# Attention with a gated layer: layernorm statistics gathered at a slot's start, one sum formed last, the output weights' sums moved to VectorE, half of the sigmoids formed later

## The chip, the cores and the metric

The kernel runs on one core of a Trainium2 chip. The metric is the device time of one execution in microseconds (us); lower is better. The kernel before was timed three times: 1114.41, 1114.5 and 1115.24 us, so the median is 1114.5 us.

## The reference

All in float32, for 4 rows of 512 tokens with 1024 features:

```python
xn = layernorm(x)                                   # no weight, no bias
q, k, v = xn @ Wq, xn @ Wk, xn @ Wv                 # 16 heads of 64; rotary on q and k
a = softmax(causal(q @ k.T) / 8) @ v
s = a @ Wo
routing = softmax(xn @ gate_w.T)                    # 8 experts
f = ((xn * (routing @ in_scale)) @ sign(weight).T) * (routing @ out_scale) + bias
out = x + s * silu(f)
```

## The kernel before, in words

**Strassen products.** Every large product is split into 2x2 blocks and done with seven block products instead of eight. For that the kernel forms sums of blocks: `form_w` (S1 to S4, of weights) and `form_x` (T1 to T4, of a row's normalized input X) for the projections, `form_a` (S1 to S4 of attention's output) and `sum_wo` (t1 to t4 of the output weights `wo`) for the output projection, `sign_sum` (T1 to T4 of the sign weights) for the gated layer. They are done on VectorE (DVE), except t3, which GpSimd (POOL) forms: `engine = nc.gpsimd if n == 3 else nc.vector` (L995). T1 of the last row is written in place over the block b12 of X, since no other place is left; the rows before have a place of their own.

**Two halves.** The first half of the program does the projections and the attention of 16 groups (4 rows b times 4 groups g), in 16 *slots*. Slot k projects group k in 84 steps (a step is one `nc.tensor.matmul`, which is two MATMUL rows in the trace), and into these steps the attention of group k-1 is woven, as a list of 16 *pieces* (`attention_pieces`, `interleave`): one piece each 5.25 steps. A group has two units, u0 and u1. The plan of pieces: 4: values of an older unit, scores of u0 and softmax of its tiles 1 and 3; 6: softmax of u0's tiles 2 and 0; 10: `transpose_blocks(u0)`; 12: values, then scores and first softmax of u1; 14: the rest of u1's softmax; 2 of the next slot: `transpose_blocks(u1)`. In the slots of g = 2 and g = 3 the next row's layernorm is woven in too: tile t0's whole layernorm at the slot's first piece, tile t0+1's at piece 7, TensorE transposes of t0 at pieces 8 and 9, of t0+1 at 13 and 14. The x tiles have two buffers; the fourth tile of a row is loaded at piece 15 of the slot of g = 2, once the buffer of tile t0+1 has been transposed.

A layernorm is two `bn_stats` (L171), `bn_aggr` (L177), a square root on ScalarE (ACT, L179), a reciprocal and the normalization on DVE (L186, L187). ACT holds one set of function tables at a time: a square root after an exponential has an ACT_TABLE_LOAD before it, and so has the next exponential.

`softmax` adds the mask (L542) and takes the maximum (L545) on DVE, exponentiates on ACT (L548), and scales on POOL (L558). `transpose_blocks` is ten transposes on DVE from p to y (L576, "the burst"), pinned in a row, and 16 DMAs from y back to p (L586), all on SyncE's (SP) queue for most units. `values` multiplies by v (L601), copies the result on ACT (L610) and stores it to at_d. `rotary` is four ACT copies (L316, L317), one DVE operation (L318) and two POOL operations (L319, L320), after the last add of a projection (`c`, L349).

**The second half** starts at L961. With the last two units still in work, the gated layer of the token pairs q = 0 and 1 (`gated`, `ffn`) is computed in pieces by `dense`, which also issues `sum_wo`; `gate` (L1021, L1022) multiplies and adds the bias, and `silu` (L1029, L1030) is a sigmoid on ACT and a product on POOL. All eight `silu` of q = 0 and 1 stand ahead of the loop over pairs. The loop does for each q: `form_a` (for q < 2), then `project_out(q)`, whose products come in the order 1 (a11 by b11), 6 (S2 by t2), 2, 7 (S3 by t3), 5 (S1 by t1), 4 (by t4), 3. It stops at four `yield`s: ahead of product 1, after product 6, after product 7, after product 5; at each, one entry of the list `ahead` is issued. For q = 0 these are the sign sums 1, 2, 3.

**What sets the order.** The order on TensorE (PE) is the program's. On the other engines a planner orders the instructions of each engine by its own estimate of when they are ready, with program order as the priority; `keep_in_program_order` pins an instruction behind the one that was issued before it on its engine. Each engine runs its list strictly in order, so a waiting instruction holds all behind it. TensorE's results lie in a ring of four PSUM banks (`bank`), shared by projections, transposed x, tile 1's scores and values; a bank is free when its readers on DVE or ACT are done.

Of the kernel before, what the change touches and what calls it, by code (L numbers as in the profile page):

```python
# [9 lines left out]
F32 = mybir.dt.float32  # L10
F32R = mybir.dt.float32r
AF = mybir.ActivationFunctionType
ALU = mybir.AluOpType
# [7 lines left out]
B, S, E = 4, 512, 1024  # L21
# [21 lines left out]
def attn_gated_ffn_kernel(  # L43
# [138 lines left out]
    def normalize(b, t):  # L182
        xt = xin[b, t]
        mv, std = MV[b, t]
        rstd = st.tile([P, 1], F32, tag="rstd", name=f"rstd_{b}_{t}")
        nc.vector.reciprocal(rstd, std)  # L186
        nc.vector.tensor_scalar(xt, xt, mv[:, 0:1], rstd, op0=ALU.subtract, op1=ALU.mult)  # L187

    def layernorm(b, t):
        half_statistics(b, t, 0)  # L190
        half_statistics(b, t, 1)
        deviation(b, t)
        normalize(b, t)

    def transpose_x(b, t, g):
        if b not in X:
# [94 lines left out]
    def form_x(b, n):  # L291
        b11, b12, b21, b22 = quarters_x(b)
        if n > 1:
            f = fp.tile([P, 4, TH], F32, tag=f"T{n}", name=f"T{n}_{b}")
        elif b < B - 1:

            f = sgp.tile([P, 4, TH], F32, tag="last", name=f"T1_{b}")
        else:

            f = b12  # L300
        TF[b, n] = f
        x0, x1 = {
            1: lambda: (b12, b11),
            2: lambda: (b22, TF[b, 1]),
            3: lambda: (b22, b12),
            4: lambda: (b21, TF[b, 2]),
        }[n]()
        nc.vector.tensor_tensor(f, x0, x1, op=ALU.subtract)
# [534 lines left out]
    def attention_pieces(k, late):  # L843

        units = [(*groups[k], i) for i in range(2)]
        w, v = late
        u0, u1 = units

        def values_and_scores(before, u):
            def both():  # L850
                if before:
                    values(before)
                scores(u)
                softmax(u, 1, 3)

            return both

        pieces = [[] for _ in range(16)]  # L860

        last = k == len(groups) - 2
        plan = {
            2: lambda: v and transpose_blocks(v),
            3 if last else 4: values_and_scores(w, u0),
            4 if last else 6: lambda: softmax(u0, 2, 0),
            8 if last else 10: lambda: transpose_blocks(u0),
            9 if last else 12: values_and_scores(v, u1),
            10 if last else 14: lambda: softmax(u1, 2, 0),
        }  # L870
        if last:
            plan[14] = lambda: transpose_blocks(u1, ordered=True)
        for n, piece in plan.items():
            pieces[n].append(piece)
        return pieces, units
# [11 lines left out]
    for k, (b, g) in enumerate(groups):  # L887
        pieces = [[] for _ in range(9)]
        if k > 0:
            pieces, late = attention_pieces(k - 1, late)  # L890

        def at(n, piece):
            pieces[n].append(piece)


        if g == 0:
            routing = [lambda n=n: router(b, n) for n in range(3)]
            if k == 0:
                at(0, routing[0])
                at(1, lambda: (load_scales(in_scale), load_scales(out_scale)))  # L900
                at(2, routing[1])
                at(4, routing[2])
                at(5, lambda: split_scales(isc))
            else:
                if b < B - 1:
                    at(5, routing[0])
                at(8, routing[1])
                at(15, routing[2])
        elif g == 1 and b + 1 < B:

            at(11, lambda: [load_x(b + 1, t) for t in range(2)])
            if b == 0:
                at(1, lambda: split_scales(osc))
        elif g > 1 and b + 1 < B:
            t0 = 2 * (g - 2)
            layernorm(b + 1, t0)
            at(7, lambda: layernorm(b + 1, t0 + 1))
            for n, t, h in ((8, t0, 0), (9, t0, 1), (13, t0 + 1, 0), (14, t0 + 1, 1)):
                at(n, lambda t=t, h=h: transpose_x(b + 1, t, h))
            if g == 2:  # L920
                at(11, lambda: load_x(b + 1, 2))
                at(15, lambda: load_x(b + 1, 3))
        if k in (5, 9, 12, 14):
            n = {5: 0, 9: 2, 12: 4, 14: 6}[k]
            at(0, lambda: (load_sign(n), load_sign(n + 1)))
            at(8, lambda: make_sign(n))
            at(15, lambda: make_sign(n + 1))
        if b == B - 1:

            if g < 2:  # L930
                load_xn(g)
            if g in (1, 2):
                at(1, lambda: in_scales(g - 1, score_banks))
            if g == 3:
                z_place[0] = [xip.tile([P, E], F32, tag="x", name=f"z0_{i}") for i in range(2)]
                at(1, lambda: out_scales(0, score_banks))
        if k == 11:

            at(15, lambda: router(b + 1, 0))
        interleave(pieces, fill, 3 * 7 * 4 if k else 3 * 7 * 4 - 8)  # L940
        if g == NGRP - 1:
            for _ in fill:
                pass
            if b + 1 < B:
                for n in (3, 1, 2, 4):
                    form_x(b + 1, n)
                fill = projections(b + 1)
    pctx.close()
# [39 lines left out]
    def sum_wo(n, c):  # L988
        out_, x0, x1 = {
            1: (t1, b12, b11),  # L990
            2: (t2, b22, t1),
            3: (t3, b22, b12),
            4: (t4, b21, t2),
        }[n]
        engine = nc.gpsimd if n == 3 else nc.vector  # L995
        difference = engine.tensor_tensor(out_[:, c, :], x0[:, c, :], x1[:, c, :], op=ALU.subtract)  # L996
        if n != 3:
            tc.keep_in_program_order(difference)

    def ffn(q, i, k):  # L1000

# [24 lines left out]
    def silu(q, i, k):  # L1026
        z = Z[q, i][:, k * HALF : (k + 1) * HALF]
        g = work.tile([P, HALF], F32, tag="g", name=f"g_{q}_{i}_{k}")
        nc.scalar.activation(g, z, AF.Sigmoid)  # L1029
        nc.gpsimd.tensor_tensor(z, z, g, op=ALU.mult)  # L1030
# [16 lines left out]

    u0, u1 = units = [(*groups[-1], i) for i in range(2)]
    w, v = late
    sums = iter([(n, c) for n in (1, 3, 2, 4) for c in range(4)])  # L1050

    def dense(gates, n, n_sums=0):
        for i in range(n):
            next(gates)
            if i < n_sums:
                sum_wo(*next(sums))
# [7 lines left out]
    dense(gates, 8)  # L1064

    split(1, 0)
    transpose_blocks(u0, ordered=True)
    load_wo(1)
    values(v)
    scores(u1)  # L1070
# [7 lines left out]
    out_scales(1, score_banks)  # L1078
    dense(gates, 2)
    transpose_blocks(u1, (nc.sync, nc.scalar), ordered=True)  # L1080
    dense(gates, 10, 10)
    values(u0)
    dense(gates, 2, 2)
    values(u1)
    for _ in gates:
        pass
# [28 lines left out]
    def sign_sum(n):  # L1115

        if n == 3:
            TS[n] = [sg[4], sg[5]]
        else:
            t = (app if n == 4 else tsp).tile(  # L1120
                [P, 2, E], F32R, tag="ap" if n == 4 else f"T{n}", name=f"Tsg{n}"
            )
            TS[n] = [t[:, r, :] for r in range(2)]
        for r in range(2):
            x0, x1 = {
                1: lambda: (sg[4 + r], sg[r]),
                2: lambda: (sg[6 + r], TS[1][r]),
                3: lambda: (sg[6 + r], sg[4 + r]),
                4: lambda: (sg[2 + r], TS[2][r]),
            }[n]()  # L1130
            nc.vector.tensor_tensor(
                TS[n][r], x0.bitcast(F32), x1.bitcast(F32), op=ALU.subtract
            )

    PARTS = {}
# [185 lines left out]
            )  # L1321

    load_xn(2)

    for q in range(2):
        for i in range(2):
            for k in range(2):
                silu(q, i, k)
    for q in range(len(pairs)):
        if q < 2:  # L1330
            for n in range(1, 5):
                form_a(q, n)
        if q == 0:
            load_at(1)
        ahead, later = [], []
        if q == 0:
            ahead = [lambda n=n: sign_sum(n) for n in (1, 2, 3)]
        elif q < len(pairs) - 1:
            ahead = [
                lambda: None,  # L1340
                lambda: (in_scales(q + 1), later.append(first_parts(q + 1))),
                lambda: out_scales(q + 1),
                lambda: later.pop()(),
            ]
        for _ in project_out(q):
            if ahead:
                ahead.pop(0)()
        if q != 1 and q + 1 < len(pairs):
            load_at(max(q + 1, 2))
        if q == 1:  # L1350
            sign_sum(4)
        if 1 <= q < len(pairs) - 1:
            gated_by_strassen(q + 1)
            if q + 2 < len(pairs):
                load_xn(q + 2)
# [58 lines left out]
```

## Time and profile before

| | |
|---|---|
| timed runs | 1114.41, 1114.5, 1115.24 us |
| profiled execution | 1114.49 us, of which its span is 1112.6 us |
| mean granted TensorE clock | 0.998 |
| busy: PE, DVE, POOL, ACT | 98%, 81%, 52%, 42% of the span |
| ACT_TABLE_LOAD for a square root (L179) | 12, of 1283 ns each |

The profile is of one execution. In the timeline view a row is a run of like instructions of one engine: start, length, engine, line, operation, output<-inputs, shapes, count, and in brackets the idle time before it with the instruction that ended it. A wait on several semaphores is put down to the one that came last, so the name in the brackets can be wrong where that one had long been done. Ends of matmuls are modelled; the distance from start to start is the safer figure.

### The profile page before, as it was taken

To read this page: it belongs to the slowest core of one execution; us is meant where nothing else is said; L and a number is where in the kernel's file an instruction comes from. 1 tells how busy PE (TensorE), PEld (TensorE's weight loads), DVE (VectorE), ACT (ScalarE), POOL (GpSimd) and SP (SyncE) were. 2 spreads that over 40 slices of the span, in tenths; PEclk is the share of its full clock that TensorE was granted. 3 is DMA by queue.
4 is the path that set the end of the run, shared out by engine and by line. 5 is a ranking of instruction groups with operands and counts; after the bars stand their busy time and mean duration, and the time that the engine had idled before them with its cause. 6 is when DMAs were issued, how large, how long until landed. Compare 5 with 4: busy or idle time off the path is not lost.

```text
span 1112.6 us, 15955 instructions
## 1 busy us (share of the span) xinstructions
PE 1086.9 (98%) x5176; PEld 788.0 (71%) x5176; DVE 896.9 (81%) x1736; ACT 469.9 (42%) x1080; POOL 575.5 (52%) x594
## 2 busy tenths in 40 slices
PE   9999999999989999998999999999979999999998
PEld 8887677787768778776877787777744545655664
DVE  7887989788897978889787987887797777667764
ACT  2553665454366545436653452664520222122220
POOL 0672555555255555525552662674585455444535
PEclk9999999999999999999999999999999999999999
DMA  9415556644655664465566544554683222431431
GB/s 322 144 60 149 174 148 159 194 136 120 178 168 155 169 177 135 120 180 168 159 169 195 171 149 141 151 131 127 165 252 114 81 91 103 156 118 47 142 114 57
DMA packets 86898, 163.88 MB, mean 147 GB/s; under 512 B 13472, under 2 KB 49056, under 8 KB 80800
## 3 DMA queue, kind: packets, MB, share of 16 engines
q1 hardware_dynamic: 80528, 152.91, 46.2%
q0 software_dynamic: 4576, 8.39, 2.2%
q10 hardware_dynamic: 1712, 1.57, 0.5%
q8 instruction: 41, 0.67, 0.3%
q14 instruction: 41, 0.34, 0.1%
HBM read 95.45 MB, written 25.43 MB: 109 GB/s over the span
## 4 chain that ended last, share of the span: by engine, by line
PE 74%; DVE 11%; POOL 4%; issue 3%; ACT 3%; DMA 2%; SPq 1%; POOLq 0%; DVEq 0%; ACTq 0%
PE pj L335 25%; PE wo L1235 16%; PE pj L422 13%; PE ff L1175 7%; PE sc L522 5%; PE pv L601 5%; POOL p L558 2%; DVE y L576 2%; DVE S L289 2%; DVE nmx L545 1%; SPq L586 1%; PE xtp L201 1%; DVE w L289 1%; DMA xn_d<-X 1%; ACT sw L317 1%
## 5 line engine op out<-in xcount | busy, mean ns | idle before, releaser
L558 POOL TENSOR_SCALAR p<-p,rs 128x256 f32<-128x256 f32 (+3 forms) x256 | 181.8, 726 | 189.0 <-DVE rs L556 144.3
L548 ACT ACTIVATE p<-sc,nmx 128x256 f32<-128x256 f32 (+3 forms) x256 | 132.8, 529 | 92.9 <-DVE nmx L545 72.6
L319 POOL TENSOR_TENSOR sw<-sw,sin_sb 128x512 f32<-128x512 f32 x64 | 89.6, 1400 | 94.4 <-ACT sw L317 93.0
L335 PE MATMUL pj<-X,w 128*128 128x256 f32 x576 | 134.4, 382 | 0.2 <-ACT X L207 0.2
L335 PE MATMUL pj<-T,S 128*128 128x256 f32 x512 | 118.2, 381 | 8.5 <-ACT v L610 7.2
L335 PEld LDWEIGHTS pj<-X,w 128*128 128x128 f32 x576 | 108.1, 190 | 18.6 <-issue 2.9
L576 DVE STREAM_TRANSPOSE y<-p 128x256 f32<-128x256 f32 x320 | 110.2, 408 | 12.7 <-POOL p L558 12.7
L316 ACT ACTIVATE sw<-c 32x512 f32<-32x512 f32 x128 | 80.3, 628 | 81.0 <-DVE c L349 79.3
L335 PEld LDWEIGHTS pj<-T,S 128*128 128x128 f32 x512 | 96.0, 190 | 23.6 <-ACT v L610 8.8
L335 PE MATMUL pj<-T,w 128*128 128x256 f32 x448 | 107.2, 382 | 0.0
L545 DVE TENSOR_REDUCE nmx<-sc 128x1 f32<-128x256 f32 (+3 forms) x160 | 104.9, 683 | 1.3
L320 POOL TENSOR_TENSOR rot<-rot,sw 128x512 f32<-128x512 f32 x64 | 94.1, 1470 | 5.0
L335 PEld LDWEIGHTS pj<-T,w 128*128 128x128 f32 x448 | 83.3, 190 | 15.2 <-issue 4.6
L422 PE MATMUL pj<-w,X 128*128 128x256 f32 x416 | 93.8, 380 | 0.0
L422 PEld LDWEIGHTS pj<-w,X 128*128 128x128 f32 x416 | 78.7, 190 | 11.0 <-issue 0.5
L542 DVE TENSOR_TENSOR sc<-sc,mask 128x256 f32<-128x256 f32 (+1 forms) x160 | 57.2, 371 | 30.8 <-PE sc L522 30.8
L317 ACT ACTIVATE sw<-c 32x512 f32<-32x512 f32 x128 | 80.4, 628 | 1.7
L522 PE MATMUL sc<-rot,rot 64*128 64x128 f32 (+3 forms) x512 | 80.3, 444 | 0.4 <-DVE v L448 0.3
L422 PE MATMUL pj<-w,T 128*128 128x256 f32 x352 | 80.2, 381 | 0.0
L610 ACT COPY v<-pv 128x512 f32<-128x512 f32 x32 | 18.6, 581 | 145.6 <-PE pv L601 132.7
L385 POOL TENSOR_TENSOR part<-part,part 128x256 f32<-128x256 f32 x32 | 25.9, 809 | 102.1 <-ACT part L384 81.8
L601 PE MATMUL pv<-p,v 128*64 128x256 f32 (+3 forms) x512 | 76.0, 439 | 2.7 <-DVE xp L996 2.7
(177 smaller groups left out, 2042.9 us busy)
## 6 DMA issues: line engine op xcount, KB each, us to landing
p<-y SPq DMA_DIRECT2D x504, 80.0 KB, 2.1
w<-in_wqk SPq DMA_DIRECT2D x31, 1024.0 KB, 5.3
w<-in_wv SPq DMA_DIRECT2D x16, 1024.0 KB, 5.2
x<-in_x SPq DMA_DIRECT2D x16, 512.0 KB, 3.5
at_d<-v SPq DMA_DIRECT2D x32, 256.0 KB, 2.7
xp<-xn_d SPq DMA_DIRECT2D x16, 512.0 KB, 4.5
ap<-at_d SPq DMA_DIRECT2D x16, 512.0 KB, 5.0
xr<-in_x SPq DMA_DIRECT2D x32, 256.0 KB, 3.0
```

The source lines that it names most:

```text
L317: nc.scalar.activation(sw[r + 32 : r + 64, :], c[r : r + 32, :], AF.Copy, scale=sc)
L319: nc.gpsimd.tensor_tensor(sw, sw, sin_sb, op=ALU.mult)
L320: nc.gpsimd.tensor_tensor(rot, rot, sw, op=ALU.add)
L335: nc.tensor.matmul(ps, lhsT=wq[:, k, :], rhs=xq[:, k, :], start=(k == 0), stop=(k == 3))
L422: nc.tensor.matmul(ps[:, j, :], lhsT=xq[:, k, j * P : (j + 1) * P], rhs=wq[:, k, :], start=(k == 0), stop=(k == 3),)
L522: nc.tensor.matmul(head(i, h), lhsT=Q[u][r : r + D, i * P : (i + 1) * P], rhs=K[u][r : r + D, : (i + 1) * P], start=True, stop=True,)
L545: nc.vector.tensor_reduce(nmx[:, hs], v, AX.X, ALU.max, negate=True)
L548: nc.scalar.activation(pt[:, h, :], ps[h], AF.Exp, bias=nmx[:, h : h + 1], accum_out=ssum[:, h : h + 1],)
L558: nc.gpsimd.tensor_scalar(pt[:, h, :], pt[:, h, :], rs[:, h : h + 1], 1.0, op0=ALU.mult, op1=ALU.mult,)
L576: nc.vector.transpose(out[:, :, :, o : o + 32], src.rearrange("p h (b c) -> p h b c", b=4))
L601: nc.tensor.matmul(by_block[r : r + D, :, 32 * j :], lhsT=V[u][:, j, r : r + D], rhs=PT[u][:, :, o : o + 32 * (TPB - j)], start=(j == 0), ...
L1235: nc.tensor.matmul(ps, lhsT=lhs[:, k, :], rhs=rhs[:, k, :], start=(first and k == 0), stop=(k == 3), skip_group_check=not first,)
```

## The change

1. Rows: in the slots of g = 2 and 3 the statistics and square roots of both tiles come at the first piece (`layernorm_scales`), the normalization of t0 right behind them, that of t0+1 at piece 3. The transposes of t0 come at pieces 7 and 8. `transpose_blocks(u0)` comes at piece 9 in all slots but the last.
2. Last row: `form_x` in the order 3, 2, 4, 1, and T2 as T3 + b11, which is the same sum, so that nothing needs T1.
3. Output weights: t3 on DVE, pinned; order 1, 2, 3, 4. In `dense` only t1 and t2 are formed; t3 between `form_a(0, 3)` and `form_a(0, 4)`, t4 after product 6 of q = 0.
4. Sigmoids and sign sums: `silu` of q = 0 after product 6 of q = 0, that of q = 1 after product 5; sign sum 1 after product 7 of q = 0, sign sums 2 and 3 at the first and fourth stop of q = 1. Sign sums are pinned. Sign sum 4 stays after q = 1.
5. The 16 DMAs of the last group's u0 alternate between SP's and POOL's queue.

```diff
-    def layernorm(b, t):
+    def layernorm_scales(b, t):
         half_statistics(b, t, 0)
         half_statistics(b, t, 1)
         deviation(b, t)
-        normalize(b, t)
...
         TF[b, n] = f
+        if b == B - 1 and n == 2:
+            nc.vector.tensor_tensor(f, TF[b, 3], b11, op=ALU.add)
+            return
...
-            8 if last else 10: lambda: transpose_blocks(u0),
+            8 if last else 9: lambda: transpose_blocks(u0),
...
-            layernorm(b + 1, t0)
-            at(7, lambda: layernorm(b + 1, t0 + 1))
-            for n, t, h in ((8, t0, 0), (9, t0, 1), (13, t0 + 1, 0), (14, t0 + 1, 1)):
+            layernorm_scales(b + 1, t0)
+            layernorm_scales(b + 1, t0 + 1)
+            normalize(b + 1, t0)
+            at(3, lambda: normalize(b + 1, t0 + 1))
+            for n, t, h in ((7, t0, 0), (8, t0, 1), (13, t0 + 1, 0), (14, t0 + 1, 1)):
...
-                for n in (3, 1, 2, 4):
+                for n in (3, 1, 2, 4) if b + 1 < B - 1 else (3, 2, 4, 1):
...
-        engine = nc.gpsimd if n == 3 else nc.vector
-        difference = engine.tensor_tensor(out_[:, c, :], x0[:, c, :], x1[:, c, :], op=ALU.subtract)
-        if n != 3:
-            tc.keep_in_program_order(difference)
+        tc.keep_in_program_order(
+            nc.vector.tensor_tensor(out_[:, c, :], x0[:, c, :], x1[:, c, :], op=ALU.subtract)
+        )
...
-    sums = iter([(n, c) for n in (1, 3, 2, 4) for c in range(4)])
+    sums = iter([(n, c) for n in (1, 2, 3, 4) for c in range(4)])
...
-    transpose_blocks(u0, ordered=True)
+    transpose_blocks(u0, (nc.sync, nc.gpsimd), ordered=True)
...
-    dense(gates, 10, 10)
+    dense(gates, 10, 4)
     values(u0)
-    dense(gates, 2, 2)
+    dense(gates, 2)
...
-            nc.vector.tensor_tensor(
-                TS[n][r], x0.bitcast(F32), x1.bitcast(F32), op=ALU.subtract
-            )
+            tc.keep_in_program_order(
+                nc.vector.tensor_tensor(
+                    TS[n][r], x0.bitcast(F32), x1.bitcast(F32), op=ALU.subtract
+                )
+            )
...
-    for q in range(2):
-        for i in range(2):
-            for k in range(2):
-                silu(q, i, k)
+    def silu_pair(q):
+        for i, k in ((0, 0), (1, 1), (1, 0), (0, 1)):
+            silu(q, i, k)
     for q in range(len(pairs)):
         if q < 2:
             for n in range(1, 5):
                 form_a(q, n)
+                if q == 0 and n == 3:
+                    for c in range(4):
+                        sum_wo(3, c)
...
         if q == 0:
-            ahead = [lambda n=n: sign_sum(n) for n in (1, 2, 3)]
+            ahead = [
+                lambda: None,
+                lambda: (silu_pair(0), [sum_wo(4, c) for c in range(4)]),
+                lambda: sign_sum(1),
+                lambda: silu_pair(1),
+            ]
         elif q < len(pairs) - 1:
             ahead = [
-                lambda: None,
+                lambda: q == 1 and sign_sum(2),
                 lambda: (in_scales(q + 1), later.append(first_parts(q + 1))),
                 lambda: out_scales(q + 1),
-                lambda: later.pop()(),
+                lambda: (later.pop()(), q == 1 and sign_sum(3)),
             ]
```

## The prediction

> **What bounds the kernel now.** I read the busy table first, then TensorE's (PE's) own waits, then the timeline around each wait on PE and on the engine that it names, last the stretches from 775 to 875 us. PE is busy for 1086.9 of 1112.6 us, so only what shortens PE's idle time can help; PE's waits, which fill few places, are the budget.
>
> The busy line of the page and PE's waits (us in total, times, longest):
> ```profile
> PE 1086.9 (98%) x5176; PEld 788.0 (71%) x5176; DVE 896.9 (81%) x1736; ACT 469.9 (42%) x1080; POOL 575.5 (52%) x594
> ```
> ```profile
> PE pj L335 <- ACT v L610: 7.2, 4, 1.9
> PE xtp L201 <- ACT p L548: 4.2, 3, 1.4
> PE wo L1235 <- ACT g L1029: 3.0, 1, 3.0
> PE pv L601 <- DVE xp L996: 2.7, 1, 2.7
> PE pj L335 <- DVE T L308: 1.3, 1, 1.3
> ```
> Three of the four waits of the first row and all of the second are pairs, in the slots of g = 2 of rows 0, 1 and 2, at 136, 330 and 525 us. The first pair on PE, then DVE and ACT in the same stretch:
> ```profile
> 135.77 2.43 PE L335 MATMUL pj<-T,S 128*128 128x256 f32 x10 [1.79 <-ACT v L610]
> 139.58 0.66 PE L201 MATMUL xtp<-ident,x 128*128 128x128 f32 x4 [1.38 <-ACT p L548]
> ```
> ```profile
> 126.79 1.03 DVE L187 TENSOR_SCALAR x<-x,mv,rstd 128x1024 f32<-128x1024 f32 x1
> 127.74 0.68 DVE L386 TENSOR_TENSOR c<-pj,part 128x512 f32<-128x512 f32 x1
> 128.34 3.37 DVE L576 STREAM_TRANSPOSE y<-p 128x256 f32<-128x256 f32 x10
> 131.64 0.38 DVE L349 TENSOR_TENSOR c<-pj,part 128x256 f32<-128x256 f32 x1
> ```
> ```profile
> 132.05 0.63 ACT L316 ACTIVATE sw<-c 32x512 f32<-32x512 f32 x1 [6.65 <-DVE c L349]
> ...
> 135.16 0.56 ACT L610 COPY v<-pv 128x512 f32<-128x512 f32 x1
> ...
> 137.66 1.28 ACT L548 ACT_TABLE_LOAD   x1
> 138.96 0.47 ACT L548 ACTIVATE p<-sc,nmx 128x256 f32<-128x256 f32 x1
> ```
> DVE runs without a gap and reaches the add `c` only at 131.64; ACT idles 6.65 us for it, then does the rotary copies ahead of the copy of v that PE waits for; then it loads the exponential's table, and PE's transpose of x waits for the exponential behind it. In the second half:
> ```profile
> 824.39 3.70 PE L1235 MATMUL wo<-wo,ap 128*128 128x512 f32 x8
> 831.12 5.37 PE L1235 MATMUL wo<-xp,S 128*128 128x512 f32 x8 [3.03 <-ACT g L1029]
> 836.32 3.60 PE L1235 MATMUL wo<-wo,ap 128*128 128x512 f32 x8
> ```
> ```profile
> 813.64 7.04 DVE L996 TENSOR_TENSOR xp<-wo,xp 128x512 f32<-128x512 f32 x3
> ...
> 825.88 3.42 DVE L1106 TENSOR_TENSOR S<-ap 128x512 f32<-128x512 f32 x2
> 829.23 1.75 DVE L1106 TENSOR_TENSOR S<-S,ap 128x512 f32<-128x512 f32 x1
> ```
> Product 6 reads S2 and t2, not a sigmoid: S2 ends at 830.97, and that is the true releaser. The eight matmuls after the wait take 836.32 - 831.12 = 5.20 us instead of 3.44, at a granted clock of 0.93 in 825 to 850 us.
>
> **The change part by part.** Idle time in brackets counts from a modelled end; start to start each wait costs about 0.16 more. The sum is made against the profiled execution: 1112.6 us of span and 1.9 around it, 1114.49, the same as the median of 1114.5.
>
> *A, rows.* Ahead of `c`, DVE does tile t0+1's two bn_stats (1.27), bn_aggr (0.20), reciprocal (0.15) and normalization (1.03), 2.65 us in all, between 119 and 128 us. They move to a place where DVE has room: it idles 2.19 us ahead of 99.50 and 2.15 ahead of 108.01. The burst moves too, but stands ahead of `c` in both orders, so it shifts `c` by nothing. `c` then comes at 131.64 - 2.65 = 129.0 (POOL's share of it, L385, is done at 127.27), the copy of v at 132.5 to 133.1. PE would need it at 135.77 - 1.95 = 133.8: the first wait is gone. The rotary copies, which now end at 137.64, end at 135.0; with both square roots in a row the table load at 137.66 falls away, so the exponential ends near 135.5, and PE asks at 139.58 - 1.95 - 1.55 = 136.1: gone too. 3 x (1.95 + 1.55) = 10.5 us. The extra square root costs ACT nothing: 12 of the 24 loads around L179 go (2 x 1.28 in each of six slots).
> What is added: in the slots of g = 3 DVE wants the fourth x tile at once. In row 0 the third's statistics end at 148.09 and the fourth lands at 148.92; in rows 1 and 2 the differences are 1.0 and 0.3, so DVE stands 2.1 us in all, with the burst, `c` and softmax behind it. It is near caught up at 159.62 (idle 0.85 before sc). Cost on PE between 0 and 2.1; I take 1.0.
>
> *The burst one piece earlier* (5.25 steps of two matmuls of 0.216 us, 2.27 us). It needs u0's p from POOL. In the slots of g = 0 and 2 p is done some 5 us ahead of it (123.22 against 128.34), in those of g = 3 2.2 us (172.13 against 174.35): no wait. In those of g = 1 DVE waits for p already (1.9 us ahead of 270.51, 3.96 ahead of 664.13) and would wait up to 2.27 longer. Behind it stand a rotary operation and the adds of v (L448) that free PE's banks; but the burst ends at about 273.8 in any order, and PE ends the product that these adds read at 275.36 - 3 x 0.43 = 274.1. Between 0 and 4 x 2.27 = 9.1; I take 0, by these rows.
>
> *B, last row's T1.* DVE waits 6.91 us ahead of 589.96 for the store of xn that reads b12; behind T1 stand T2 and T4, and PE's S2-by-T2 product starts 1.42 late. In the new order T2 and T4 run in that gap, T1 at 589.96 to 591.2; its product is the fourth block product, due after 592.8. Gain 1.4.
>
> *C, the same slot at 627.73* (the fourth wait on the copy of v, 2.02): no layernorm here to remove. DVE is 2.5 us earlier after B, PE 1.4, and DVE idles 1.31 at 609.22 on the way. Between 0 and 2.0; I take 0.5, nearer to the row at 609.22.
>
> *F, output weights.* t3's four sums on POOL stand at 814.09 to 819.52, and beside them DVE's first two t2 sums take 4.74 and 1.77 us; those alone take 0.68. New: the burst ends at 813.7, four t2 sums 2.7, one gate 0.7, S1, S3, S2 at 0.68 to 1.75 each: S2 by 819 to 822. PE's product 1 still starts at 824.39, product 6 is due at 827.93: no wait, and no low clock. Gain 3.19 + 1.76 = 4.95. t3 (4 sums) follows S3, 2.7 to 7 us, due at product 7, 834.8. t4 is pinned behind u2, the add that follows product 6 (831.4), 2.7 to 7 us, so 834 to 838.5, due at product 4, 841.7; behind t4 on DVE stand the first finish and u3, whose bank PE wants only after product 4. Sign sum 1 follows u3 at 838; sums 2 and 3 (1.22 each half, 4.9 us) fall into 845 to 870 on the new clock, where DVE is busy for 15.5 of 25 us and nothing of PE waits on them before product 6 of the gated layer at 880. The sigmoids' POOL work moves behind product 6: finishes want it, PE doesn't.
>
> *E, values of u1 at 822.09, and the queue.* The [2.68 <- DVE xp L996] here is a wrong name: the last y-to-p DMA lands at 821.68. Its chain (scores, softmax, burst at 810.34, 16 DMAs) is left as it is, gain 0. What is new in it: 8 DMAs of u0 are issued by POOL, ahead of u1's scaling on the same queue. Near row: POOL's four issues at 809.40 take 2.17, 0.54 each, beside DVE's burst. 8 x 0.54 = 4.3 from 795.8 on, and POOL idles until 800.02 anyway:
> ```profile
> 800.02 1.44 POOL L558 TENSOR_SCALAR p<-p,rs 128x256 f32<-128x256 f32 x2 [6.45 <-DVE rs L556]
> ```
> So 0.1 late, and POOL is done 2.1 us ahead of the burst. [...]
>
> Sum: 10.5 - 1.0 + 1.4 + 0.5 + 4.9 = 16.3; 1114.5 - 16.3 = **1098.2**.
>
> **The rivals.** *Half of the rows' gain.* The burst now stands ahead of adds that free PSUM banks (`c` L386), 3.37 us longer; scores of u1 need such a bank at about 132.6 and it came free at 128.42, a margin of 4.2, in the last row 3.3. The planner may also keep the square roots apart, so that a load stays. For it: in the last row the scores of u1 wait for `c` already (0.5 us, and 3.26 us long at 621.99 against 2.43). Against it: `c` is not moved by the burst. Half of A: +5.2, 1103.4.
>
> *VectorE the bound in 813 to 845.* Eight more sums of 0.68 to 1.75 us, 5 to 14 us, pinned in a stretch where DVE is busy 25.00 of 25 us. If t4 or S2 comes late, F is given back: +4.9, 1103.1. Against it: sign sums 2 and 3, 9.1 us of that stretch, go.
>
> *The POOL queue* (slower). If the issues cost more than (4.2 + 2.1) / 8 = 0.8 us each, u1's scaling, burst and DMAs are late, and values of u1 has nothing behind which to hide. [...] Decides from 2.8 us each (16.3 + 6.3 over 8).
>
> *It doesn't do what it says*: the planner's order brings the same waits back; 1114.
>
> **How the numbers follow.** Forecast 0.60, half of rows 0.18, VectorE 0.12, queue 0.07, no effect 0.03. About 0.2% (2.2 us) is what a measurement of this kernel can tell from no change. Faster 0.60 + 0.18 + 0.12 = 0.90, slower 0.07, same 0.03. Low end: x waits cost nothing (-1.0), all of C (-1.5), E closes too (-2.8): 1092.9, so 1093. High end: the two partial rivals are near 1103, and with a third of the 9.1 us of the burst's waits 1106; beyond lie the queue and no effect.
>
> **What would show it.** Right: no pair of waits near 133, 325 and 516 us; 6 loads at L179 instead of 12; T1 behind T4; one sum of t2 near 0.7 us; product 6 right behind product 1 and clock 1.0 there; the wait of about 2.7 at values of u1 still there. Wrong: DVE waiting on x<-in_x for over 1 us with PE behind it; POOL issues over 0.8 us; PE waiting for t4, or for a bank at scores of u1.

## The result, and the profile after

The changed kernel takes 1110.06 us, the median of six runs (1109.29 to 1112.66), beside 1115.77 for the kernel before in the same comparison; the ratio of the means is 0.9955, with a 95% interval of 0.9942 to 0.9968. It is faster, by 0.45%. Forecast were 1098.2 and a range of 1093 to 1106: the sign was right and the size was not. In the profiled executions the span falls from 1112.6 to 1108.0 us, by 4.67 of the 16.3 us of the sum.

First the busy line of the page, then those of PE's waits on which the argument rests (us in total, times, longest), both of the changed kernel. Code lines are a few higher than before: the copy of v is L613, the exponential L551, `c` L352.
```profile
PE 1086.5 (98%) x5176; PEld 787.9 (71%) x5176; DVE 885.8 (80%) x1740; ACT 456.7 (41%) x1068; POOL 564.0 (51%) x598
```
```profile
PE pj L338 <- ACT v L613: 8.5, 7, 2.4
PE pv L604 <- POOL z_t L1027: 2.7, 1, 2.7
PE ff L1182 <- DVE cf L1197: 0.9, 1, 0.9
PE pj L338 <- ACT p L551: 0.7, 2, 0.4
PE pj L425 <- ACT p L551: 0.5, 1, 0.5
```
The transposed x no longer waits for an exponential (4.2 before), the output weights no longer wait (3.0), nor does the product of T1 (1.3). But the wait for the copy of v, which step A was to end, has grown from 7.2 to 8.5 us, and three names are new: `ff` for `cf`, and `pj` twice for an exponential.

Where it went can be followed by the same matmul's start in both traces. Up to 568 us, in rows 0 to 2, PE gains 3.55 us where A counted 9.5; at the last row's T1 1.73 (B, forecast 1.4); in the slot that follows 0.33 (C, 0.5); at 718 us it loses 2.08 that no step had; between 786 and 854 it gains 3.37 (F, 4.95); at 884.6 it loses 1.01. The start is 0.56 and the tail 0.66 us longer; together that is the 4.67.

The slot of the first pair, PE and then ACT, after the change:
```profile
135.53 2.42 PE L338 MATMUL pj<-T,S 128*128 128x256 f32 x10 [1.21 <-ACT v L613]
```
```profile
129.75 0.63 ACT L319 ACTIVATE sw<-c 32x512 f32<-32x512 f32 x1 [4.02 <-DVE c L352]
...
133.61 0.62 ACT L319 ACTIVATE sw<-c 32x512 f32<-32x512 f32 x1
134.24 0.62 ACT L320 ACTIVATE sw<-c 32x512 f32<-32x512 f32 x1
134.89 0.59 ACT L613 COPY v<-pv 128x512 f32<-128x512 f32 x1
135.50 0.47 ACT L551 ACTIVATE p<-sc,nmx 128x256 f32<-128x256 f32 x1
```
ACT begins the rotary at 129.75 instead of 132.05, 2.3 us earlier: DVE's `c` came early, as A has it, and the table load is gone. The copy of v starts at 134.89 instead of 135.16, 0.3 earlier. In the kernel before five rotary copies stood ahead of it; now it is all eight, three more at 0.63.

### The profile page after: what moved, and what is told of

Same layout as the page of the kernel before. It is cut to its first block, busy times and chain, and to the rows that moved or that the text cites. A ratio compares the mean times of both kernels' runs of the same rounds, so it can differ in the third digit from the quotient of the medians.

```text
span 1108.0 us, 15954 instructions
## 1 busy us (share of the span) xinstructions
PE 1086.5 (98%) x5176; PEld 787.9 (71%) x5176; DVE 885.8 (80%) x1740; ACT 456.7 (41%) x1068; POOL 564.0 (51%) x598
## 5 line engine op out<-in xcount | busy, mean ns | idle before, releaser
L561 POOL TENSOR_SCALAR p<-p,rs 128x256 f32<-128x256 f32 (+3 forms) x256 | 185.2, 740 | 199.7 <-DVE rs L559 134.1
L551 ACT ACTIVATE p<-sc,nmx 128x256 f32<-128x256 f32 (+3 forms) x256 | 132.9, 529 | 111.4 <-DVE nmx L548 83.0
L322 POOL TENSOR_TENSOR sw<-sw,sin_sb 128x512 f32<-128x512 f32 x64 | 85.2, 1331 | 79.4 <-ACT sw L320 74.0
L323 POOL TENSOR_TENSOR rot<-rot,sw 128x512 f32<-128x512 f32 x64 | 90.8, 1419 | 5.0
L613 ACT COPY v<-pv 128x512 f32<-128x512 f32 x32 | 18.8, 586 | 146.2 <-PE pv L604 132.6
```

The source lines that it names most:

```text
L322: nc.gpsimd.tensor_tensor(sw, sw, sin_sb, op=ALU.mult)
L323: nc.gpsimd.tensor_tensor(rot, rot, sw, op=ALU.add)
L551: nc.scalar.activation(pt[:, h, :], ps[h], AF.Exp, bias=nmx[:, h : h + 1], accum_out=ssum[:, h : h + 1],)
L561: nc.gpsimd.tensor_scalar(pt[:, h, :], pt[:, h, :], rs[:, h : h + 1], 1.0, op0=ALU.mult, op1=ALU.mult,)
```

## The experiments

My theory from these rows: the change altered the planner's order on ACT, and that order took back A's gain. The rival: the burst that now stands ahead of the adds, or a bank that they free, holds PE. Each run has its own runs of the kernel before on the same chip; their medians were 1116.1 us (e1 to e4), 1114.9 (e5, e8, e10, e11) and 1115.0 (e6, e12 to e14). Ratios are to these. A wait given without a row is from start to start, less the usual distance.

**The copy of v placed by hand** (`e1_v_first`). `issue_after` puts what is issued inside it behind the named instruction on the same engine.

```diff
+        behind = nullcontext()
+        if copies_of_v and m == 1 and u[2] == 1:
+            behind = tc.issue_after(copies_of_v[-1])
+        with behind:
             for r in range(0, P, 64):
                 nc.scalar.activation(sw[r : r + 32, :], c[r + 32 : r + 64, :], AF.Copy, scale=sc)
```

> The changed kernel, with one thing more: the four ACT copies of the second rotary of m = 1 are placed behind the copy of v in ACT's order. Theory (ACT's order): in the changed kernel the add c is early, but all eight rotary copies (5.1 us) stand ahead of the copy of v, so PE still waits at 135.5, 329.4, 522.9 and 718.1 us; with the copy after four of them v is there at 132.9 instead of 135.5, the four waits (1.4 + 1.5 + 1.5 + 2.0 = 6.4) go, that at 622.7 shrinks by 0.6: 1110.1 - 7.0 = 1103. Rival (the burst of transposes ahead of the adds, or a bank, holds PE): the copy comes early and PE still waits at the same places: 1110. Between them, if the exponentials behind the rotary become late by the 0.6 of the copy: 1104 to 1106.

1103.71 us, ratio 0.9901 (0.9883 to 0.9919). The waits at 135, 329, 523 and 718 us are gone, that at 622 is 2.01 instead of 2.52. ACT's order was the releaser that mattered. In return the waits for an exponential grow: 1.58, 0.50, 0.87, 0.46 and 1.36 at 162, 305, 354, 497 and 546 us, 4.8 in all, where the changed kernel had 0.64, 0.55, 0.31, 0.46 and 0.30, 2.3 in all.

**The same in the kernel before** (`e2_before_v_first`, the same edit).

> The kernel before, with the same placing of the second rotary behind the copy of v and nothing else. Theory: the pair of waits needs both, c early and the copy of v ahead; alone the copy moves from 135.16 to 134.6 at the best, and PE then waits for the exponential behind the rotary and the table load as before, so the pairs give 0 to 1.6 us in all: 1114 to 1116. Rival (ACT's order alone was the bound, moving the layernorm was never needed): the three first waits and that at 627.7 go, 1.95 each: 1108.

1115.35 us, ratio 0.9997 (0.9986 to 1.0007): nothing. The copy moves to 134.58, as worked out, and the first wait of each pair shrinks from 1.96 to 1.45 us start to start. The second grows from 1.55 to 2.19, since it ends with the exponential behind rotary and table load, which starts at 139.05 as against 138.96:
```profile
PE xtp L201 <- ACT p L553: 6.1, 3, 2.0
PE pj L339 <- ACT v L615: 5.7, 4, 1.9
```
Before, these two were 4.2 and 7.2. So A was needed; order alone gives nothing.

**The burst back at piece 10** (`e3_burst_10`).

```diff
-            8 if last else 9: lambda: transpose_blocks(u0),
+            8 if last else 10: lambda: transpose_blocks(u0),
```

> The changed kernel with the burst of u0 back at piece 10. If the burst's earlier place causes the new wait at 718.1 (2.0) and the three new bank waits at 162.7, 306.5 and 499.9 (0.64 + 0.55 + 0.46): 1110.1 - 3.6 = 1106.5. If ACT's order causes the first and the statistics of two tiles at once the others, the burst's place is worth nothing: 1110, within 1. If the earlier place gave room that the prediction did not count: above 1112.

1104.14 us, ratio 0.9898 (0.9881 to 0.9915). None of the three cases had this; they all left the first waits of 135, 329 and 523 us where they were. It is as good as placing the copy by hand. What happens is seen on ACT:
```profile
129.49 0.63 ACT L319 ACTIVATE sw<-c 32x512 f32<-32x512 f32 x1 [4.50 <-DVE c L352]
...
132.06 0.63 ACT L319 ACTIVATE sw<-c 32x512 f32<-32x512 f32 x1
132.60 0.56 ACT L613 COPY v<-pv 128x512 f32<-128x512 f32 x1
133.18 0.63 ACT L320 ACTIVATE sw<-c 32x512 f32<-32x512 f32 x1
...
135.11 0.47 ACT L551 ACTIVATE p<-sc,nmx 128x256 f32<-128x256 f32 x1
```
Five copies stand ahead of the copy of v again; it starts at 132.60, and no pair of waits is left. In ACT's order as built this holds in six slots, those of g = 2 in all four rows and of g = 0 in rows 1 and 2: five ahead with the burst at piece 10, all eight at piece 9. They are the slots of the waits at 135, 329, 523 and 718 us, and of two of 0.35 at 233 and 426. The burst is DVE's, and the copies are ACT's; they are tied only through the planner, which orders by its own estimate of when things are ready. So the two theories were one: the burst's place sets ACT's order. What in the estimate tips it is not shown.

**u0's DMAs on one queue** (`e4_one_queue`, `transpose_blocks(u0, ordered=True)`).

> The changed kernel with all 16 DMAs of the last group's u0 on SP's queue. The trace of the changed kernel shows POOL's issues at 0.49 us each, and E's wait as long as before (2.7), so neither queue is on the path: 1110, within 1. If two queues brought u0's values and with them u1's scaling forward: 1112 to 1114. If POOL's issues did cost, hidden in the rest: 1108.

1109.85 us, ratio 0.9949 (0.9934 to 0.9964): the second queue neither costs nor gains. POOL's eight issues in the changed kernel, count, busy time and mean:
```profile
L589 POOL DMA_DIRECT2D p<-y x8 | 4.0, 509 | 2.8 <-issue 2.8
```

**Part 1 without the burst, in the kernel before** (`e8_rows`: `layernorm_scales`, the normalizations and the transposes of x as in the diff).

> The kernel before with part 1 of the change alone, without the earlier burst: both tiles' statistics at the first piece, normalization of t0+1 at piece 3, transposes at 7 and 8. In ACT's order five rotary copies then stand ahead of the copy of v, as in the kernel before. Theory (step A was right in its gain and short in its price): the three pairs go, 10.5, and the bank waits at 162, 305, 354, 498 and 546 us that the other kernels show (4.5 in all) come: 1116.1 - 6.0 = 1110. Step A as predicted (10.5 - 1.0): 1106.6. Rival (the rows bring nothing without the rest): 1115.

1108.14 us, ratio 0.9937 (0.9919 to 0.9955). Both forecasts took 1116.1 for the kernel before, which ran at 1114.9 here: as gains they were 6.0 and 9.5, and 6.8 is measured (5.0 to 9.0 by the interval). So the price was short, as the theory has it. The three pairs are gone, and waits for an exponential of 1.91, 0.50, 0.42, 1.19 and 0.40 us, 4.4 in all, stand in the five places.

**Parts 3, 4 and 5 alone** (`e11_second`).

> The kernel before with parts 3, 4 and 5 of the change alone (sums of output weights, sigmoids and sign sums, two queues). Step F as predicted (3.19 + 1.76): 1111.1. Theory (the wait of 3.2 goes, the low clock is drawn anew at E's wait, and the pinned sign sum 4 costs 1.0 at the product that waits for cf): 1116.1 - 3.2 + 1.0 = 1113.9, with 1.7 less in the executions that keep the full clock at E. Rival (VectorE is now the bound in the output weights and gives F back): 1116.

1112.85 us, ratio 0.9981 (0.9972 to 0.9990). The wait ahead of product 6 is gone, E's is 2.81, and the new one for `cf` is 1.09, at 885.7. The gain of 2.1 is what the theory had, 2.2; VectorE does not give F back.

**Idle transposes in E's wait** (`e5_warm`).

```diff
     dense(gates, 2)
+    keep_warm(12)
     values(u1)
```

> The changed kernel with twelve TensorE transposes of the identity (0.16 us each, 1.9 in all) ahead of the values of u1, in the 2.7 us in which PE has nothing to do; they compute nothing that is used. Theory (the low clock of 3.41 us is granted after a window in which PE mostly idled, and falls on E's wait in some executions): no low clock behind E, 1.7 less in those executions: median 1108.4 to 1109.3, and a narrower spread than 1109.3 to 1112.7. Rival (the low clock has another source, a load on the chip or the length of the whole run): 1110, the same spread. If the transposes' bank comes late or they end after the DMAs: 1111.

1109.99 us, ratio 0.9960 (0.9946 to 0.9975), from 1108.77 to 1111.17. The low clock behind E is gone in the profiled execution. It came at 623.9 us instead, after the wait of slot C. The median stands still, against the theory's 1108.4 to 1109.3; where the low clock fell in the other executions is not recorded. They list mean clocks of 0.997 to 1.000, those of the changed kernel 0.996 to 0.998. Stretches of 820 to 824 us, first the changed kernel, then this one (length, busy us of PE, PEld, DVE, ACT, POOL with counts, granted clock, DMA share, GB/s):
```profile
820.00:824.00 4.00, 4.00 (x19) 1.88 (x16) 3.23 (x6) 0.86 (x2) 0.00 (x0) 0.71 0.02 4
```
```profile
820.00:824.00 4.00, 3.26 (x18) 1.75 (x19) 4.00 (x7) 0.83 (x2) 0.48 (x1) 1.00 0.23 66
```

**The normalization of t0+1 later**, in the kernel with the burst at piece 10. First only asked for later (`e10_norm_7`, `at(7, ...)` for `at(3, ...)`), then pinned there as well (`e14_norm_pinned`: `keep_in_program_order` on the reciprocal of rows b > 0, odd tiles).

> The changed kernel with the burst of u0 at piece 10 and the normalization of t0+1 at piece 7 instead of 3. With the normalization at piece 3 the kernel took 1104.1, and PE waited 4.5 us in five places for an exponential that frees a bank. Theory (the normalization ahead of the softmax, 1.0 to 1.6 us of DVE in the slots of g = 3, makes the exponential late): the waits at 162.8, 354 and 546 shrink by 1.0 to 1.6 in all of them that have as much: 1104.1 - 2 = 1102. Rival (the wait for the fourth x tile makes them): 1104. If the normalization then falls ahead of the add c again: three times 1.0 and more back, 1107.

1106.18 us, ratio 0.9933 (0.9917 to 0.9949). This decides nothing: the planner still put the normalization ahead of the softmax, four of the five waits stayed (2.08, 0.60, 1.12, 0.59), and the profiled execution had four low-clock windows.

> The changed kernel with the burst of u0 at piece 10 and the normalization of t0+1 pinned at piece 7, so that on DVE it now really stands behind the softmax of u0 (unpinned, at piece 7, it stood ahead of it still). Theory (0.8 to 1.6 us of normalization ahead of the softmax make the exponential late that frees a bank): the waits at 162.8 (1.9), 305.9 (0.4), 354 (0.4), 498.3 (1.3) and 546.5 (0.4) shrink by 0.8 to 1.6 where they have as much: 3.4 us less, 1101. Rival (the x tile that lands late, or the forms of weights, make them): 1104. If the normalization now stands ahead of the add c: waits at 131 to 136 come back, 1105 or more.

1103.48 us, ratio 0.9897 (0.9883 to 0.9912). The exponential's waits shrink from 4.5 us to 0.7. But `c` comes later, the copy of v with it: waits of 0.66, 0.66 and 0.84 come at 135, 327 and 519 us, each with a second of 0.25 behind it. From 565 us on PE's matmuls start within 0.14 us of those of `e3_burst_10`: all of it is given back.

That the normalization was the cause is shown at 498 us, where the masks of the softmax start 1.08 us earlier and PE stands 0.27 instead of 1.33. At 162.8, the longest of the waits, it is a part at most. The table load ahead of the exponential starts 0.33 earlier than the 160.90 of `e3_burst_10` (shown below):
```profile
160.57 1.28 ACT L553 ACT_TABLE_LOAD   x1 [3.31 <-DVE nmx L550]
```
PE, held up at 135 and 137, arrives 1.2 later, and that is most of the 1.5 by which this wait shrinks.

**Sign sum 4 unpinned** (`e6_sign4`, `if n != 4` ahead of the pin).

> The changed kernel with sign sum 4 no longer pinned. Theory (two halves of 1.72 us in a row hold u2 of the gated layer back by 1.0, and with it the gate, the sigmoid ahead of the cast of S4, and cf): its halves go between the finishes again, the wait of 0.9 (1.08 start to start) at 884.6 us is gone, 1110.1 - 1.1 = 1109.0. Rival (the wait comes because PE is 6 us earlier and DVE's chain of finishes isn't): it stays, 1110.

The wait for `cf` is gone. The time is 1110.49 us, ratio 0.9958 (0.9941 to 0.9975), no less: this profiled execution had two low-clock windows (1.7 us each, see the last section) where the changed kernel's had one. Matmul by matmul, PE is 1.33 us behind the changed kernel ahead of that place and 0.35 behind it afterwards: 0.98 is gained there, near the forecast 1.1, and the medians don't show it.

**The copy of v ahead in the last row's first slot** (`e12_c_v_first`, with the burst at piece 10; the condition of `e1_v_first` is `m == 1 and u[0] == B - 1 and u[1] == 0`).

> The changed kernel with the burst of u0 at piece 10, and in the last row's first slot both rotaries of m = 1 placed behind the copy of v. Theory (the wait of 2.0 at 619.8 us is set by five rotary copies ahead of the copy of v, whose input is there 1.3 us before the add c): the copy runs at 617 instead of 619.2 and the wait is gone: 1104.1 - 2.0 = 1102, or 1.7 less still in executions that got a low clock there. Rival (the wait goes over to the exponentials behind the rotary, 0.6 later, or to the bank of the next product): 1103 to 1104.

1103.07 us, ratio 0.9887 (0.9872 to 0.9902). The wait for the copy of v is gone; 1.12 us come back at 621.4, where PE waits for the exponential behind the rotary, as the rival has it. The ratio's interval overlaps that of `e3_burst_10`. In that kernel's trace four rotary copies stand ahead of the copy of v here, not the five that I had counted.

**All together** (`e13_best`).

> All together: burst of u0 at piece 10, second rotaries and those of the last row's first slot behind the copy of v, sign sum 4 not pinned, normalization of t0+1 pinned at piece 7, u1's 16 DMAs over three queues, eight idle transposes ahead of u1's values. If the single gains add up from 1104.1: 2.0 for the copy of v, 1.1 for the sign sum, 1.1 for the third queue, 0 to 3.4 for the normalization, and no low clock: 1096 to 1100.

1100.79 us (1100.22 to 1102.12), ratio 0.9871 (0.9857 to 0.9885), the lowest time of the study, with a span of 1098.7 us, and above the forecast 1096 to 1100. PE's two costliest waits:
```profile
PE xtp L202 <- ACT p L558: 2.2, 3, 0.7
PE pv L611 <- POOL z_t L1035: 1.8, 1, 1.8
```
The transposed x waits again: against PE's own matmuls `c` is as late as in `e14_norm_pinned`, and what the first waits no longer take the second ones do (0.73 us each in the idle time). The three queues, forecast at 1.1, gave nothing: with the queue chosen by a modulo 3, SP still had eight of u1's sixteen DMAs and took 5.77 us for them (4.97 with two queues), and from the last product's start to the values of u1 it is 3.07 us (3.05 with two).

## Why the prediction was wrong, step by step

**The burst one piece earlier: 0, and this is the step that failed.** The bounds were 0 to 9.1 us, and I took 0, because DVE's queue shows nothing that the burst makes late. The runs with the burst at 9 and at 10 stand at 1110.06 and 1104.14: it costs 5.9 us (by the profiled spans 6.6, or 4.9 without the low-clock window that only the first had). Not by the wait for p on which the bound was built, but through the planner, which placed the copy of v behind three more rotary copies of 0.63 us, on an engine on which the burst doesn't run. With the burst at 10 the result would have stood inside the range, though still 6 us above the forecast; the rest is below.

**A, the rows.** The mechanism was right: `c` at 129.3 (forecast 129.0), six loads at L179 instead of 12. "The copy of v at 132.5 to 133.1" assumed ACT's order of before; with that order it starts at 132.60 and the exponential ends near 135.5, as worked out (`e3_burst_10`), and both waits of each pair are gone, 10.5 us. With the new order only the second waits went; the first shrank from 1.96 to 1.37, 1.55 and 1.55, and one of 1.97 came at 718.1. The price was the second step that failed: I took 1.0, for the fourth x tile. Free of the other waits the rows cost 4.5, and two things make it. The normalization now stands ahead of the softmax, a move I had costed at nothing since DVE had room:
```profile
154.45 1.59 DVE L187 TENSOR_SCALAR x<-x,mv,rstd 128x1024 f32<-128x1024 f32 x1
...
160.90 1.28 ACT L551 ACT_TABLE_LOAD   x1 [4.81 <-DVE nmx L548]
162.20 0.47 ACT L551 ACTIVATE p<-sc,nmx 128x256 f32<-128x256 f32 x1
```
```profile
162.81 3.50 PE L425 MATMUL pj<-w,X 128*128 128x256 f32 x15 [1.78 <-ACT p L551]
```
These are DVE and ACT, then PE, of `e3_burst_10`, in the slot of g = 3 of row 0: the exponential frees a bank for which PE stands 1.78 us.

And DVE waits for an x tile, in slots that I had not counted. In the slots of g = 2 it now wants the row's second tile at once too. In rows 1 and 2 that tile's buffer is first held by a weight tile until its signs are formed, so its load is issued only at the slot's start. The queue and DVE, in the changed kernel:
```profile
290.40 0.33 SPq L161 DMA_DIRECT2D x<-in_x  x1
```
```profile
293.94 1.29 DVE L171 BATCH_NORM_STATS2 bn<-x 128x6 f32<-128x512 f32 x2 [1.64 <-DMA x<-in_x]
```
At 487.38 it is 1.55. The kernel before issued these loads at 291.22 and 485.67 and read the tiles only from 313 and 508 us on, so its trace had it to read. In the slots of g = 3, where I had expected 2.1 us, the changed kernel's DVE doesn't stand for x. My sign "DVE waiting on x<-in_x for over 1 us with PE behind it" came true: with the same order on DVE, the wait at 485 us is 2.42 in `e3_burst_10`, 2.28 in `e8_rows` and 1.56 in `e12_c_v_first`, and PE's wait at 498 is 1.33, 1.18 and 0.47, each 1.1 less than DVE's. How the 4.5 us divide between the two is not settled.

**B** was right in size: no wait is left there. But T1 does not stand behind T4, as my sign had it, since the planner put it ahead: DVE still waits 3.88 us for T1's place at 584.84, then forms T4 at 585.99, early enough.

**C** came near in size, 0.33 for 0.5, but by luck. The wait grew from 2.02 to 2.52: four rotary copies stood ahead of the copy of v before and five do now, and from the first of them to it are 2.57 and 3.10 us. What is gained are the scores ahead of it, which take 2.43 us instead of 3.26.

**E and the queue** were right: 2.86 against 2.84 us start to start, and an issue on POOL takes 0.51 us. The queue's rival had 7 in 100, and no run shows the price of 2.8 us an issue from which it would decide: the eight issues take 4.0 us together, and with all of u0's DMAs on one queue (`e4_one_queue`) the kernel takes 1109.85 us beside 1110.06.

**F** was right in the wait and wrong in the clock. The sums of t2 take 0.67 us each, S2 ends at 820.13, and product 6 follows product 1 at once:
```profile
819.15 3.93 PE L604 MATMUL pv<-p,v 128*64 128x512 f32 x16 [2.69 <-POOL z_t L1027]
823.01 3.70 PE L1242 MATMUL wo<-wo,ap 128*128 128x512 f32 x8
826.55 3.60 PE L1242 MATMUL wo<-xp,S 128*128 128x512 f32 x8
```
3.19 us are gained. The 1.76 of low clock I had bound to the wait ahead of product 6. In the runs it stands behind other waits too (last section): the profiled execution after has it behind E, where the values of u1 hold PE for 3.86 us until the next product starts (2.30 before).

**Sign sum 4** I left out: pinned, its halves run in a row, 1.22 us and then 2.32, the second begun beside POOL's sum (1.22 each before), and hold u2 of the gated layer back by 1.0.
```profile
874.06 3.45 DVE L1137 TENSOR_TENSOR Tsg<-sg,Tsg 128x1024 fp32r<-128x1024 f32 x2
877.44 0.68 DVE L1205 TENSOR_TENSOR part_ff<-ff,part_ff 128x512 f32<-128x512 f32 x1
```
The product before it ends about 876.2; u2, the gate, the sigmoid and the cast behind it all come 1.0 late, and PE waits 0.92 for `cf`. `e6_sign4` shows it.

The rival "the planner's order brings the same waits back" had 3 in 100. That is what happened to four of the seven waits, the three first ones of the pairs, shorter by 0.4 to 0.6, and C's, and it brought one more at 718 us. The chance was far too small for a kernel whose order is written down on one engine alone. "Half of the rows' gain" came nearer to the rows' number, 3.55 of 9.5, but not by its mechanism: with the burst still at piece 9 but the copy of v ahead (`e1_v_first`) the first waits are gone, so no bank behind the burst held PE there. My range ended at 1106, since it allowed the burst a third of its bound and did not add that to a price of A that was too low.

## What to carry to other kernels

Where a planner orders the engines, moving work on one engine can reorder another: a move is not costed until the order that it produces on the engine ahead of the bound has been read, or the instruction that the bound waits for has been pinned. Two waits in a row that end with the same engine can be one wait: in `e2_before_v_first` what the first lost the second took. And a gain on an engine with room has to be followed to the operation that it now stands ahead of, and so has an input that is wanted earlier to the load that brings it: here the softmax paid for a second normalization and for a tile whose buffer was not yet free.

## What the runs showed of the hardware

In the fourteen profiled executions, between the program's first and last microseconds, the granted clock is halved for one window of 3.41 us at a time (once for two in a row): it is 0.50 from 831.43 to 834.84 us in the kernel before and from 818.93 to 822.34 in the changed kernel, and 1.00 in the window ahead of each. In each of these traces the changes of the clock lie whole multiples of 3.41 us apart: from the end of that window to the change near the program's end it is 276.48 us before (81 windows) and 283.31 after (83). I divided each trace along its own grid, from 10 us to the last two windows, and took PE's idle share of each window. The next window was at half clock after shares of 0.56 and above (0.89 before, 0.72 after, and eleven more), and not after 0.53 and below (at most 0.52 before, 0.51 after), with one exception that stays open: in `e10_norm_7` two low windows in a row follow windows of 0.37 and 0.22. In the window at 623 us of `e6_sign4` PE falls 1.7 us behind the changed kernel. So of two waits of the same length one had a window at half clock behind it and one had none, by where the grid lay: E's wait of 2.68 us before had none (0.52 in its window), that of 2.69 after had one (0.72).

It goes with the spread, and is not all of it. In one comparison the kernel before takes 1117.4 us at a mean clock of 0.991 and 1114.0 at 0.998, but also 1114.0 at 0.995 and 1116.8 at 0.991, and 0.007 of the clock over the whole span would be 7.8 us, where the times differ by 3.4. The best version, whose longest idle stretch in a window is 0.43, lists 0.999 and 1.000, and its four times lie within 1.9 us. So I estimate, from the 1.7 us of one such window, that removing a wait which has one behind it is worth up to 1.7 us more than its length; how much of that reaches a median is not shown.
